# A GNN and FFN kernel on one Trainium2 core: the order of additions, weight loads and a branch around the last projection block and the last stores

## The chip, the cores and the metric

The kernel runs on one core of one Trainium2 chip. The metric is the time of the device in microseconds (us); lower is better. The engines carry these names in the profile: PE is TensorE's matrix multiply and PEld its weight load, DVE is VectorE, ACT is ScalarE, POOL is GpSimd, SP is SyncE, which here issues most of the DMAs. The "span" of a profiled execution goes from its first to its last instruction. L594 means line 594 of the kernel before.

## What is computed

Four residual stages over 1250 nodes with 1024 features each. The reference, cut to its frame:

```python
x = x + _L0_gnn_ref(_layernorm(x), W, a_l, a_r, src, dst)       # graph attention, 4 heads
x = x + _L0_ffn_ref(_layernorm(x)[None], maker, up, w_cproj)[0] # block-diagonal up, gelu, 16384 -> 1024
x = x + _L1_gnn_ref(_layernorm(x), edge_index, W, b)            # graph convolution
x = x + _L1_ffn_ref(_layernorm(x)[None], w1s, w2s, w3s, W1, W2, W3, Wg)[0]  # shared expert + best of 8
```

The second stage ends in `h @ w_cproj.T`, a product of 1250 x 16384 by 16384 x 1024 in float32. It takes most of the time. The third stage begins with `x @ W.T + b`. In the fourth, `shared = gelu(x @ w1s) * (x @ w2s) @ w3s` is added for every node, and to it the output of the one expert that the node chose.

## The kernel before

**The projection.** The long product is cut along its 16384 hidden features into 16 blocks (`NB`), and each block is multiplied by a two-level Strassen-Winograd scheme: 7 outer products, each of 7 inner ones. One step of the loop over `steps` is one product. In blocks 0 to 14 a step has 8 matrix multiplies (L594). Its result lies in one of two PSUM buffers (`po2`), ACT copies it to SBUF (L603, in `accumulate`) into one of five rotating buffers (`parts`, which the profile shows as `low`), and POOL adds it by an accumulating DMA to an array in DRAM, `acc_d` (L607). `acc_d[p, i]` thus gathers inner product i of outer product p over blocks. The operands are sums of weights and of hidden features, which DVE forms (L587, `add_up`).

**The last block.** It has 28 steps, four for each outer product p, which come in the order `OUTER` = 1, 2, 6, 7, 4, 5, 3. Each step takes two pairs of operands, so 16 multiplies. Three things happen beside them:

- `load_sums(p)` brings the seven sums of outer product p back from DRAM with seven DMAs on SP (L622, 313 KB each). `sums_of` names the step at which each p is loaded, counted from the block's first step (`end`): -13, -6, 1, 5, 12, 15, 20. Buffers for them come from those that the operands and the rotating copies leave free.
- `outer_sums(p)` is a generator of seven DVE additions (L629), which turn the seven inner sums into the four quarters of outer product p.
- `combine(p, i, po)` adds the step's PSUM result to that quarter (L643), and combines quarters of several p into the result `xT` (L648). It frees the PSUM buffer. As there are two, the products of step k+2 wait for the combine of step k.

In what order DVE meets additions and combines is decided by the loop: at each step, before the combine of the step before, it pulls two additions from the list `fill` (nine at every fourth step of the last block). A scheduler then fixes the order on each engine, in which each engine runs its instructions one after another.

**Weights of the convolution.** From step 14 of block 15 in the program's order, the sixteen pieces of the third stage's weights (`W3`, 256 KB each) are loaded by POOL (L749) whenever an operand buffer is free, and its bias by L751. The loads are in POOL's queue together with the accumulating DMAs. `W3` is read by `linear` (L775). The transposes of the first tile of nodes, by which the third stage begins (L153, L679), stand among the last products.

**The end.** The experts' outputs are copied from PSUM (L990) and stored by SP to `ys_d` in DRAM. Then a flag is loaded on every engine (L1003), and a branch (L1004) treats the case that an expert was chosen by more nodes than it has room for. With these inputs it is not taken. After the branch POOL gathers each node's expert output (L1040, ten tiles of 125 nodes, `yg` <- `ys_d`). For each tile, `project` multiplies the shared expert's hidden layer by w3s (L998, eight PE records, two PSUM buffers `po7`), DVE adds it to X (L1001), adds X to `yg` (L1046), and SP stores `yg` in two parts (L105, L106).

Of the kernel before, what the change touches and what calls it, by code (L numbers as in the profile page):

```python
# [1 line left out]

# [95 lines left out]
def gnn_ffn_kernel(ctx, tc, x, src, dst, gat_w, a_l, a_r, maker, up, cproj,  # L98
# [439 lines left out]
    with ExitStack() as tail:  # L538
# [61 lines left out]
        def accumulate(b, p, i, po):  # L600
            part = YS[parts[0]]
            parts.append(parts.pop(0))
            nc.scalar.copy(part, po[:, :, :NQ])  # L603
            if b == 0:
                nc.gpsimd.dma_start(acc_d[p - 1, i - 1], part)
            else:
                nc.gpsimd.dma_start(out=acc_d[p - 1, i - 1], in_=part, accum_op=ALU.add)  # L607

        def late_tile(t):
            xn = scratch[:R, (4 + t % 2 * 2) * 512:][:, :D]  # L610
# [7 lines left out]
        def load_sums(p):  # L618

            for i in (2, 3, 4, 5, 1, 6, 7):  # L620
                acc[p, i] = early.pop() if early and p in (1, 2, 4) else place_y(True)
                nc.sync.dma_start(YS[acc[p, i]], acc_d[p - 1, i - 1])  # L622

        def outer_sums(p):

            a = {i: acc.pop((p, i)) for i in INNER}
            for d, x, op, y in ((2, 1, ALU.add, 2), (6, 1, ALU.add, 6), (7, 6, ALU.add, 7), (4, 7, ALU.subtract, 4),
                                (6, 6, ALU.add, 5), (3, 6, ALU.add, 3), (5, 7, ALU.add, 5)):
                tt(YS[a[d]], YS[a[x]], YS[a[y]], op=op)  # L629
                yield  # L630
            for i, j in (("11", 2), ("12", 3), ("21", 4), ("22", 5)):
                acc[p, i] = a[j]
            for j in (1, 6, 7):
                free_acc(a[j])
# [5 lines left out]

        def combine(p, i, po):
            v = YS[acc[p, i]]
            tt(v, po[:, :, :NQ], v, op=ALU.add)  # L643
            a = {q: acc[q, i] for q in OUTER if (q, i) in acc}
            for d, x, op, y in {2: (("11", 1, ALU.add, 2),), 6: ((6, 1, ALU.add, 6),), 7: ((7, 6, ALU.add, 7),),
                                4: (("21", 7, ALU.subtract, 4),), 5: (("22", 7, ALU.add, 5), (5, 6, ALU.add, 5)),
                                3: (("12", 5, ALU.add, 3),)}.get(p, ()):
                tt(output(d, i) if isinstance(d, str) else YS[a[d]], YS[a[x]], YS[a[y]], op=op)  # L648
            for q in {2: (2,), 6: (1,), 4: (4,), 5: (7, 6), 3: (5, 3)}.get(p, ()):
                free_acc(acc.pop((q, i)))  # L650
# [44 lines left out]
        later = dict(zip((33, 36, 38, 40, 42, 44, 46, 48), pieces))  # L695
        late = {1: 5, 2: 6, 3: 7, 4: 8, 5: 9}
        end = (NB - 1) * 49
        last, j, fill, sums_of = None, 0, [], dict(zip((end + v for v in (-13, -6, 1, 5, 12, 15, 20)), OUTER))
        norm = {}
        for n, (b, p, i, pairs) in enumerate(steps):  # L700
            m = n - 49 * b
# [28 lines left out]
                if m in later:  # L730
                    hidden(b + 1, *later[m])
            assert n != end - 13 or all(v < 33 for k, v in buf.items() if k[1] == "X")
            if n in sums_of:
                load_sums(sums_of[n])
                fill.append(outer_sums(sums_of[n]))
            if n == end:
                blocks.close()
                tl = rest.enter_context(tc.tile_pool(name="tl", bufs=2))
# [1 line left out]
                yh += parts  # L740
            if b == NB - 1:
                if m >= 14 and len(W3) < 2 * KD:
                    for g in range(2):
                        for k in range(KD):
                            at = [v for v in xw if not 8 <= v < 16]
                            if at and (k, g) not in W3:
                                xw.remove(at[0])
                                W3[k, g] = XS[at[0]].rearrange("p q o -> p (q o)")
                                nc.gpsimd.dma_start(W3[k, g], gcn_w[k * P:(k + 1) * P, g * 512:(g + 1) * 512])  # L749
                if m == 23:  # L750
                    nc.gpsimd.dma_start(bias, gcn_b.partition_broadcast(R))  # L751
                while m >= 16 and len(fetched) < 4 and fetch(len(fetched)):
                    pass
                if m == 22:
                    add_out(0)
                    level(0)
                if m == 24:
                    turn_tile(0)
                if m == 27:
                    add_out(1)  # L760
                    level(1)
            po = product(pairs)
            for _ in range(9 if n >= end and m % 4 == 3 else 2):
                if n > end - 9 and fill and next(fill[0], 0) == 0:
                    fill.pop(0)
            if last:
                (combine if last[0] == NB - 1 else accumulate)(*last[last[0] == NB - 1:])
            last = b, p, i, po
        combine(*last[1:])

# [99 lines left out]
    with back_end:  # L870
# [120 lines left out]
                        nc.sync.dma_start(ys_d[:NE * ROWS, :].rearrange("(p s) d -> s p d", s=NS)[e * (ROWS // P) + s][:m], y[:m])  # L991

        with tc.tile_pool(name="ops7", bufs=2, space=PSUM) as ops:
            def project(dst, w3t, h, t):
                po = ops.tile([R, 2, 512], F32, name="po7")
                for f in range(2):
                    for g in range(2):
                        nc.tensor.matmul(po[:, g, :], h[:, f, t * R:(t + 1) * R],  # L998
                                         w3t[:, f, g * 512:(g + 1) * 512], start=(f == 0), stop=(f == 1))
                xs = X[:, t, :]  # L1000
                nc.vector.tensor_tensor(xs, po.rearrange("p a b -> p (a b)"), xs, op=ALU.add)  # L1001

            if_late = nc.values_load(flag[0:1, 0:1], min_val=0, max_val=1)  # L1003
            with tc.If(if_late > 0):  # L1004
                with tc.tile_pool(name="lw", bufs=1) as lwp, tc.tile_pool(name="lps", bufs=1, space=PSUM) as lps:
                    for e in range(NE):
                        a, b, c = w1[e], w2[e], w3[e]
                        w12 = lwp.tile([P, 2, KD, F], F32, name="lw12")
                        w3t = lwp.tile([P, 2, D], F32, name="lw3")
                        nc.sync.dma_start(w12[:, 0], a.rearrange("(k p) f -> p k f", p=P))  # L1010
                        nc.sync.dma_start(w12[:, 1], b.rearrange("(k p) f -> p k f", p=P))
                        nc.sync.dma_start(w3t, c.rearrange("(k p) o -> p k o", p=P))
                        mask = lwp.tile([P, N], F32, name="mask")
                        for t in range(T):
                            pb = lps.tile([P, R], F32, name="lpb")
                            nc.tensor.transpose(pb, late[:, t, e:e + 1].to_broadcast([R, P]), ident[:R, :R])
                            nc.scalar.copy(mask[:, t * R:(t + 1) * R], pb)
                        h = lwp.tile([P, 2, N], F32, name="lhid")
                        for f in range(2):
                            for n0, nn in NCH:  # L1020
                                ps = []
                                for i in range(2):
                                    pab = lps.tile([P, 512], F32, name=f"lpab{i}")
                                    for k in range(KD):
                                        nc.tensor.matmul(pab[:, :nn], w12[:, i, k, f * P:(f + 1) * P],
                                                         xT5[:, k, n0:n0 + nn], start=(k == 0), stop=(k == KD - 1))
                                    ps.append(pab)
                                g = lwp.tile([P, 417], F32, name="lg2")
                                nc.scalar.activation(g[:, :nn], ps[0][:, :nn], AF.Gelu)
                                nc.vector.tensor_tensor(g[:, :nn], g[:, :nn], mask[:, n0:n0 + nn], op=ALU.mult)  # L1030
                                nc.vector.tensor_tensor(h[:, f, n0:n0 + nn], ps[1][:, :nn], g[:, :nn], op=ALU.mult)
                        for t in range(T):
                            project(X, w3t, h, t)

            out_t = out.rearrange("(t p) d -> t p d", p=R)
            with tc.tile_pool(name="yg", bufs=T) as ygp:
                ygs = []
                for t in range(T):
                    yg = ygp.tile([R, D], F32, name="yg")
                    nc.gpsimd.indirect_dma_start(  # L1040
                        out=yg, out_offset=None, in_=ys_d,
                        in_offset=bass.IndirectOffsetOnAxis(ap=back[:, t:t + 1], axis=0))
                    ygs.append(yg)
                for t in range(T):
                    project(X, wsh[1], hs, t)
                    nc.vector.tensor_tensor(ygs[t], ygs[t], X[:, t, :], op=ALU.add)  # L1046
                    dma(nc.sync, out_t[t], ygs[t])


# [29 lines left out]
```

## Time and profile before

| what | value |
|---|---|
| time, median of 3 runs | 2980.59 us (2980.43 to 2981.76) |
| profiled execution, its own time | 2978.19 us |
| its span, mean granted PE clock | 2976.5 us, 0.993 |
| busy: PE, DVE, ACT, POOL | 2900.6, 1595.5, 874.9, 764.3 us |
| step of the last block on PE | 4.22 us (16 multiplies of 128x313) |
| one addition on DVE (L629, L643) | 0.81 us |
| accumulating DMAs (L607), issue to landing | 735 of 313 KB, median 5.9 us |
| gathers (L1040), issue to landing | 10, 7.7 / 11.8 / 19.0 us (least, median, most) |

The table by stages lists the busy time of each engine within a stretch, then PE's granted clock, the share of the 16 DMA engines and the bytes moved. In this view of the profile, the stretch from 2200 to 2250 us is the first part of the last block:

```profile
core 0: us, PE busy (x) PEld busy (x) DVE busy (x) ACT busy (x) POOL busy (x), PEclk, DMA share, GB/s
...
2150.00:2200.00 50.00, 49.86 (x225) 32.04 (x224) 29.07 (x43) 23.30 (x35) 19.57 (x26) 1.00 1.02 243
2200.00:2250.00 50.00, 35.55 (x128) 25.07 (x127) 35.02 (x45) 0.00 (x0) 2.28 (x4) 0.86 0.45 137
2250.00:2300.00 50.00, 50.00 (x191) 35.87 (x190) 32.22 (x43) 0.00 (x0) 3.23 (x6) 1.00 0.51 154
```

Around the branch the profile shows these records (PEldq and DVEq are the engines' sequencers; durations in ns, then the time of the start):

```profile
L1004 PEldq COMPARE_BRANCH  x1: 3645/3645/3645, 2927.8 to 2927.8; - x1
L1004 DVEq COMPARE_BRANCH  x1: 68/68/68, 2930.8 to 2930.8; - x1
L1004 PEldq EVENT_SEMAPHORE  x1: 51/51/51, 2931.5 to 2931.5; - x1
L1004 DVEq EVENT_SEMAPHORE  x1: 21/21/21, 2933.6 to 2933.6; - x1
```

### The profile page before, as it was taken

Reading aid. Unit: us, or ns where it says so; the run is one execution under the profiler, and the core shown is the slowest. Engines: PE = TensorE matmul, PEld = TensorE weight load, DVE = VectorE, ACT = ScalarE, POOL = GpSimd, SP = SyncE. Lnnn points to the kernel's source line nnn. Section 1 sums busy time; section 2 is a strip of 40 time slices with the busy share of each in tenths; the row PEclk is TensorE's granted clock in tenths of the full one; section 3 lists DMA queues with packets and bytes.
Section 4 is the critical chain, followed back from the end, with each engine's and each line's share of the span. In section 5 each row is a group of like instructions: output and inputs, shape, how many; then the busy total and the mean of one; then the engine's idle time right before and its main releaser. Section 6 shows DMA issues by size and latency. Waiting matters only on the chain. (4 is left out here: it accounts for less than half of the span.)

```text
span 2976.5 us, 32458 instructions
## 1 busy us (share of the span) xinstructions
PE 2900.6 (97%) x11479; PEld 1914.0 (64%) x11479; DVE 1595.5 (54%) x2611; ACT 874.9 (29%) x1415; POOL 764.3 (26%) x982
## 2 busy tenths in 40 slices
PE   8999899999999999999999999999989999999998
PEld 5574677666766766766766766766757544445774
DVE  7686987846646646646646646645556431221214
ACT  1221234444344344344344344344320110000000
POOL 2010000234434434434433434434320000002001
PEclk9999999999999999999999999999999999999999
DMA  5245523569999999999999999999983202212654
GB/s 141 65 118 140 152 66 125 186 165 172 198 170 172 199 172 170 198 172 171 197 173 171 197 172 171 197 173 148 226 226 115 74 0 74 62 56 85 211 198 164
DMA packets 252548, 449.57 MB, mean 151 GB/s; under 512 B 48160, under 2 KB 132218, under 8 KB 251753
## 3 DMA queue, kind: packets, MB, share of 16 engines
q0 software_dynamic: 115216, 270.53, 53.0%
q1 hardware_dynamic: 137162, 176.86, 19.9%
q8 instruction: 96, 1.57, 0.2%
q14 instruction: 74, 0.61, 0.1%
HBM read 175.38 MB, written 271.89 MB: 150 GB/s over the span
## 5 line engine op out<-in xcount | busy, mean ns | idle before, releaser
L607 POOL DMA_DIRECT2D acc_d<-low x686 | 594.3, 867 | 904.9 <-ACT low L603 875.4
L603 ACT COPY low<-po 128x626 f32<-128x626 f32 x735 | 500.4, 681 | 996.4 <-PE po L594 821.2
L594 PE MATMUL po<-X,arena 128*128 128x313 f32 x2176 | 613.7, 429 | 0.1
L594 PEld LDWEIGHTS po<-X,arena 128*128 128x128 f32 x2176 | 408.3, 190 | 173.4 <-issue 19.9
L594 PE MATMUL po<-low,arena 128*128 128x313 f32 x1552 | 440.2, 429 | 14.4 <-DVE arena L643 14.4
L594 PEld LDWEIGHTS po<-low,arena 128*128 128x128 f32 x1552 | 291.4, 190 | 137.0 <-DVE arena L643 14.9
L594 PE MATMUL po<-X,first_w 128*128 128x313 f32 x840 | 240.0, 428 | 0.0
L594 PE MATMUL po<-X,BZ 128*128 128x313 f32 x720 | 207.3, 431 | 0.0
L594 PEld LDWEIGHTS po<-X,first_w 128*128 128x128 f32 x840 | 157.6, 189 | 66.5 <-issue 6.8
L848 PE MATMUL ph<-low,first_w 125*125 125x512 f32 x400 | 173.6, 593 | 1.4 <-issue 1.4
L594 PEld LDWEIGHTS po<-X,BZ 128*128 128x128 f32 x720 | 135.7, 191 | 57.5 <-issue 7.5
L587 DVE TENSOR_TENSOR X<-X 128x626 f32<-128x626 f32 x141 | 114.2, 812 | 100.2 <-PE po L594 99.8
L594 PE MATMUL po<-low,first_w 128*128 128x313 f32 x560 | 160.6, 429 | 0.0
L209 PE MATMUL pz<-W,xT 128*125 128x512 f32 x320 | 141.2, 595 | 0.2 <-PEq L322 0.2
L594 PE MATMUL po<-low,BZ 128*128 128x313 f32 x480 | 138.4, 428 | 0.0
L848 PEld LDWEIGHTS ph<-low,first_w 125*125 125x125 f32 x400 | 74.2, 188 | 94.8 <-issue 94.8
L594 PEld LDWEIGHTS po<-low,first_w 128*128 128x128 f32 x560 | 104.6, 190 | 44.2 <-issue 5.5
L587 DVE TENSOR_TENSOR X<-low,X 128x626 f32<-128x626 f32 x101 | 82.0, 816 | 83.8 <-PE po L594 81.6
L587 DVE TENSOR_TENSOR low<-X 128x626 f32<-128x626 f32 x102 | 82.8, 815 | 69.4 <-PE po L594 69.1
L587 DVE TENSOR_TENSOR X<-X,low 128x626 f32<-128x626 f32 x92 | 75.1, 818 | 80.4 <-PE po L594 80.1
L277 PE MATMUL pc<-os,od 125*125 125x417 f16 (+1 forms) x588 | 110.9, 345 | 5.0 <-issue 5.0
L448 PE MATMUL po<-BZ,w 125*125 125x257 f32 x400 | 96.6, 401 | 18.7 <-DVE w L446 17.4
(263 smaller groups left out, 3407.2 us busy)
## 6 DMA issues: line engine op xcount, KB each, us to landing
acc_d<-low POOLq DMA_DIRECT2D x735, 313.0 KB, 5.9
arena<-in_cproj SPq DMA_DIRECT2D x148, 256.0 KB
w<-in_w SPq DMA_DIRECT2D x16, 1024.0 KB
BZ<-in_cproj SPq DMA_DIRECT2D x56, 256.0 KB
first_w<-in_cproj SPq DMA_DIRECT2D x52, 256.0 KB
nm<-nm_d SPq DMA_DIRECT2D x20, 546.9 KB
w3t<-in_w SPq DMA_DIRECT2D x8, 1024.0 KB
X<-acc_d SPq DMA_DIRECT2D x21, 313.0 KB
```

Source lines behind the costliest of these rows:

```text
L209: nc.tensor.matmul(pz, xT[:, k, t * R:(t + 1) * R], W[g][:, k], start=(k == 0), stop=(k == KD - 1))
L277: nc.tensor.matmul(pc[:, b, :nn], od[:, d - near[c][0], :], os[:, n0:n0 + nn], start=(c == win[d][0]), stop=(c == win[d][-1]))
L448: nc.tensor.matmul(po[i], w[:, i * R:(i + 1) * R], Z[h // 2][:, s, h % 2, :], start=(s == 0), stop=(s == T - 1))
L587: tt(view(k), *a, op=ALU.add if sign == "+" else ALU.subtract)
L594: nc.tensor.matmul(po[:, o, :NQ], view(x)[:, q, o * P:(o + 1) * P], view(y)[:, q, :], start=(i == q == 0), stop=(i + 1 == len(pairs) and q ...
L603: nc.scalar.copy(part, po[:, :, :NQ])
L607: nc.gpsimd.dma_start(out=acc_d[p - 1, i - 1], in_=part, accum_op=ALU.add)
L848: nc.tensor.matmul(pa[:, g, :], cs[:, c, :], Hs[:, c, g * 512:(g + 1) * 512], start=(c == 0), stop=(c == T - 1))
```

## The change

Three parts.

1. *Additions of the last block's sums.* The list `fill` and its loop are gone. A list `bring` says for each outer product from which step on its additions run, and how many per step: from -9 two, 0 two, 3 two, 10 four, 14 four, 18 three, 22 three, for p in the order `OUTER`. They come after the step's combine in the program, and for steps after `end` they are tied behind it: `tc.issue_after(added[-1])` places what is within it after the last combine's L643 in the order of the engine. The fourth sum (p=7) is loaded at step 7 instead of 5.
2. *Weights of the convolution.* The loads of `W3` are placed after the last accumulating DMA (`sent[0]`).
3. *The overflow branch.* The load of the flag and the branch stand after the gathers, the projections and the stores. `project` gets the place that it adds to as an argument. Within the branch, the late nodes' output is added to `ygs` instead of X, and all tiles are stored once more.

```diff
-                nc.gpsimd.dma_start(out=acc_d[p - 1, i - 1], in_=part, accum_op=ALU.add)
+                sent[:] = [nc.gpsimd.dma_start(out=acc_d[p - 1, i - 1], in_=part, accum_op=ALU.add).ins]
...
-            tt(v, po[:, :, :NQ], v, op=ALU.add)
+            added.append(tt(v, po[:, :, :NQ], v, op=ALU.add).ins)
...
-        last, j, fill, sums_of = None, 0, [], dict(zip((end + v for v in (-13, -6, 1, 5, 12, 15, 20)), OUTER))
+        last, j = None, 0
+        loads_at = dict(zip((end + v for v in (-13, -6, 1, 7, 12, 15, 20)), OUTER))
+        bring = [(end + v, k, outer_sums(w)) for v, k, w in zip((-9, 0, 3, 10, 14, 18, 22), (2, 2, 2, 4, 4, 3, 3), OUTER)]
+        added, sent = [], []
...
-            if n in sums_of:
-                load_sums(sums_of[n])
-                fill.append(outer_sums(sums_of[n]))
+            if n in loads_at:
+                load_sums(loads_at[n])
...
-                    for g in range(2):
-                        for k in range(KD):
+                    for g, k in [(g, k) for g in range(2) for k in range(KD)]:
+                        with tc.issue_after(sent[0]):
...
             po = product(pairs)
-            for _ in range(9 if n >= end and m % 4 == 3 else 2):
-                if n > end - 9 and fill and next(fill[0], 0) == 0:
-                    fill.pop(0)
             if last:
                 (combine if last[0] == NB - 1 else accumulate)(*last[last[0] == NB - 1:])
+            for n0, k, sums_of in bring:
+                if n0 <= n:
+                    with tc.issue_after(added[-1]) if n > end else nullcontext():
+                        for _ in range(k):
+                            next(sums_of, None)
...
-            def project(dst, w3t, h, t):
+            def project(w3t, h, t, dst):
...
-                xs = X[:, t, :]
-                nc.vector.tensor_tensor(xs, po.rearrange("p a b -> p (a b)"), xs, op=ALU.add)
-
-            if_late = nc.values_load(flag[0:1, 0:1], min_val=0, max_val=1)
-            with tc.If(if_late > 0):
...
-                            project(X, w3t, h, t)
+                nc.vector.tensor_tensor(dst, po.rearrange("p a b -> p (a b)"), dst, op=ALU.add)
...
-                    project(X, wsh[1], hs, t)
+                    project(wsh[1], hs, t, X[:, t, :])
                     nc.vector.tensor_tensor(ygs[t], ygs[t], X[:, t, :], op=ALU.add)
                     dma(nc.sync, out_t[t], ygs[t])
+
+                if_late = nc.values_load(flag[0:1, 0:1], min_val=0, max_val=1)
+                with tc.If(if_late > 0):
...
+                            for t in range(T):
+                                project(w3t, h, t, ygs[t])
+                    for t in range(T):
+                        dma(nc.sync, out_t[t], ygs[t])
```

The order of each engine's instructions after the change can be known without running it, and the prediction uses it.

More of the change, by code (lines that the diff above doesn't have):

```diff
@@ L1 @@
-from contextlib import ExitStack
+from contextlib import ExitStack, nullcontext
 import concourse.bass as bass
@@ L999, in project @@
                                          w3t[:, f, g * 512:(g + 1) * 512], start=(f == 0), stop=(f == 1))
-                xs = X[:, t, :]
-                nc.vector.tensor_tensor(xs, po.rearrange("p a b -> p (a b)"), xs, op=ALU.add)
-            if_late = nc.values_load(flag[0:1, 0:1], min_val=0, max_val=1)
[L1004 to L1032, printed above, removed]
-                            project(X, w3t, h, t)
@@ L1044, in gnn_ffn_kernel @@
                 for t in range(T):
-                    project(X, wsh[1], hs, t)
+                    project(wsh[1], hs, t, X[:, t, :])
                     nc.vector.tensor_tensor(ygs[t], ygs[t], X[:, t, :], op=ALU.add)
                     dma(nc.sync, out_t[t], ygs[t])
+                if_late = nc.values_load(flag[0:1, 0:1], min_val=0, max_val=1)
+                with tc.If(if_late > 0):
+                    with tc.tile_pool(name="lw", bufs=1) as lwp, tc.tile_pool(name="lps", bufs=1, space=PSUM) as lps:
+                        for e in range(NE):
+                            a, b, c = w1[e], w2[e], w3[e]
+                            w12 = lwp.tile([P, 2, KD, F], F32, name="lw12")
+                            w3t = lwp.tile([P, 2, D], F32, name="lw3")
+                            nc.sync.dma_start(w12[:, 0], a.rearrange("(k p) f -> p k f", p=P))
+                            nc.sync.dma_start(w12[:, 1], b.rearrange("(k p) f -> p k f", p=P))
+                            nc.sync.dma_start(w3t, c.rearrange("(k p) o -> p k o", p=P))
+                            mask = lwp.tile([P, N], F32, name="mask")
+                            for t in range(T):
+                                pb = lps.tile([P, R], F32, name="lpb")
+                                nc.tensor.transpose(pb, late[:, t, e:e + 1].to_broadcast([R, P]), ident[:R, :R])
+                                nc.scalar.copy(mask[:, t * R:(t + 1) * R], pb)
+                            h = lwp.tile([P, 2, N], F32, name="lhid")
+                            for f in range(2):
+                                for n0, nn in NCH:
+                                    ps = []
+                                    for i in range(2):
+                                        pab = lps.tile([P, 512], F32, name=f"lpab{i}")
+                                        for k in range(KD):
+                                            nc.tensor.matmul(pab[:, :nn], w12[:, i, k, f * P:(f + 1) * P],
+                                                             xT5[:, k, n0:n0 + nn], start=(k == 0), stop=(k == KD - 1))
+                                        ps.append(pab)
+                                    g = lwp.tile([P, 417], F32, name="lg2")
+                                    nc.scalar.activation(g[:, :nn], ps[0][:, :nn], AF.Gelu)
+                                    nc.vector.tensor_tensor(g[:, :nn], g[:, :nn], mask[:, n0:n0 + nn], op=ALU.mult)
+                                    nc.vector.tensor_tensor(h[:, f, n0:n0 + nn], ps[1][:, :nn], g[:, :nn], op=ALU.mult)
+                            for t in range(T):
+                                project(w3t, h, t, ygs[t])
+                    for t in range(T):
+                        dma(nc.sync, out_t[t], ygs[t])
```

## The prediction

> **What bounds the kernel now.** The page gives TensorE 97% of the 2976.5 us span, so I did not ask which engine is busy but where TensorE is not. First the groups of instructions: almost every product group has an idle time of 0.0 or 0.1 us, one has 14.4.
>
> ```profile
> L594 PE MATMUL po<-low,arena 128*128 128x313 f32 x1552 | 440.2, 429 | 14.4 <-DVE arena L643 14.4
> ```
>
> Then the timeline of PE around it. Columns: start, duration, instruction, and in brackets the idle time before it with its releaser.
>
> ```profile
> 2200.58 1.22 PE L594 MATMUL po<-X,BZ 128*128 128x313 f32 x4
> 2216.24 2.46 PE L594 MATMUL po<-low,arena 128*128 128x313 f32 x4 [14.45 <-DVE arena L643]
> 2218.49 1.91 PE L594 MATMUL po<-X,arena 128*128 128x313 f32 x4
> 2220.24 1.22 PE L594 MATMUL po<-low,arena 128*128 128x313 f32 x4
> 2221.29 1.22 PE L594 MATMUL po<-X,arena 128*128 128x313 f32 x4
> 2222.35 1.22 PE L594 MATMUL po<-low,first_w 128*128 128x313 f32 x4
> ```
>
> The reader is to see two losses: the gap, and after it groups of 2.46 and 1.91 us where 1.22 is normal. This step took 2222.35 - 2216.24 = 6.11 us; the others take 4 x 1.055 = 4.22. Next, why L643 was late: VectorE's timeline.
>
> ```profile
> 2200.59 1.66 DVE L629 TENSOR_TENSOR X<-X 128x626 f32<-128x626 f32 x2 [8.58 <-DMA X<-acc_d]
> 2202.79 1.73 DVE L629 TENSOR_TENSOR X<-X 128x626 f32<-128x626 f32 x2 [0.55 <-DMA X<-acc_d]
> ...
> 2214.66 0.81 DVE L629 TENSOR_TENSOR X<-X 128x626 f32<-128x626 f32 x1
> 2215.38 0.80 DVE L643 TENSOR_TENSOR arena<-po,arena 128x626 f32<-128x626 f32 x1
> ```
>
> The first combine had its product at about 2197.5, but runs at 2215.38, behind L629 additions that wait for loads. On the engine's order 16 of them stand between the last L587 addition for the first step and this combine: five of p=2, six of p=6, five of p=7. Those loads are late for a reason on POOL, whose timeline is next.
>
> ```profile
> 2175.48 0.86 POOL L607 DMA_DIRECT2D acc_d<-low  x1 [1.25 <-ACT low L603]
> 2186.40 0.58 POOL L749 DMA_DIRECT2D arena<-in_gcn_w  x1 [10.06 <-DVE arena L587]
> ...
> 2199.78 0.87 POOL L607 DMA_DIRECT2D acc_d<-low  x1 [2.57 <-DMA arena<-in_gcn_w]
> ```
>
> A W3 load waits 10.06 us for VectorE with the last seven accumulations behind it; the last goes out at 2199.78. Five loads of p=6 need those accumulations landed, as they reuse their buffers.
>
> The windows table shows no other such place: from 2250 to 2920 us PE is busy nearly throughout. So time won here is not given back on the way, and the next place that counts is the tail:
>
> ```profile
> 2933.76 36.02 PE L998 MATMUL po<-w3s,hs 128*125 128x512 f32 x80 [4.23 <-DVEq L1004]
> ```
>
> [...] 2.46 us against 1.22 after the 14.45 us gap. [...] accumulations and loads crowd one another, windows 2150 to 2200 have a DMA share of 1.02, and accumulations land after 7.3 us there, 5.9 over the kernel. [...] The trace has DVE's compare at 2930.8 and its next event at 2933.6, 2.8 us; PE's compare lasts 3.645 us.
>
> **The change, part by part.** Sums are made against the profiled execution's 2978.19 us (span 2976.5). The median of the runs is 2.40 us higher, and I subtract the same gain from it.
>
> *Additions behind combines.* Nothing is removed: 49 additions of 0.81 us stay. In the changed order on DVE the first combine goes ahead of the last five L629 of p=2, and no addition of p=6 precedes combine 2. PE's steps end at 2197.4, 2201.8, 2206.0, 2210.2, 2214.4; step k+2 needs combine k. Combine 0 is done by about 2198.3, needed at 2201.8. Then the third sum of p=2 waits for a load (2200.6 as before, if not earlier), four additions of 0.81 end at 2203.9, combine 1 at 2204.7, needed at 2206.0. Three additions and combine 2 end at 2207.9, needed at 2210.2.
> Now the critical one: the first addition of p=6 stands before combine 3 and waits for the load into the buffer that the very last accumulation used. That accumulation goes out at about 2194.1 (product ends 2193.0, ACT copy 0.68, hand-over 0.4), lands 6 to 7.3 us later at 2200 to 2201.4; the load then needs 4 to 8 us on crowded engines: 2205 to 2209. VectorE gets there at 2208.7, does four operations (3.3 us), and combine 3 ends at 2212.8, needed at 2214.4. So the load may land at about 2210 without a pause. Later steps carry two to four additions (at most 3.2 us), a combine (0.8) and up to two L648; I find slack of 1.7 to 3 us at the tightest (steps 10 and 15).
> Gain: the gap of 14.45 plus the slow clock, 6.11 - 4.22 = 1.89: **16.3 us**. If the load is late, the pause is its lateness, 0 to 4 us, plus 1.9 if the clock falls. Below nothing: the load order moves as well (the fourth sum's seven loads two steps, 8.4 us, later), but its first use is step 10, some 13 us after.
>
> *W3 behind the last accumulation.* It is this that brings the last accumulation from 2199.78 to about 2194.1; taken into the sum above. On POOL all seven accumulations now precede the sixteen L749 issues (0.54 to 0.6 us each) and the bias. W3 is first used by L775 at about 2331, more than 130 us after the first eight loads went out in the trace of before (2186 to 2197), so their delay of up to 8 us is hidden; the later ones wait for buffers as before. About seven W3 loads then meet the p=6 loads on the 16 engines (256 KB; by the page's queue table 176.86 MB took 19.9% of the span, so 0.9 us each): at most 6.3 us, which is the upper end of the lateness above.
>
> *Overflow branch behind the stores.* It was not taken: it costs the flag's load, the compare and the jump. PE no longer waits 4.23 us, nor restarts slowly (the first four weight loads are 0.86 us apart, not 0.43: 1.7 us). By the changed order half of tile 0 fills the 1.32 us hole ahead of the last expert's second half (L987 at 2925.86), so that ends 0.3 us later. But the next limit is near. The gathers (L1040) wait for the last ys_d store, not for the branch: gather 0 went out at 2935.06, landed at 2942.98; now 2943.4. DVE's order is X0, X1, yg0, X2, yg1, yg2, X3, and po7 has two buffers: tile 4's products wait for X2, which stands behind yg0. X2 ends at 2943.4 + 2 x 1.2 = 2945.8; yg2 waits for gather 2 (2948.9), so X3 ends at 2951.3, tile 5 starts there, and five tiles of 3.43 end at 2968.5 where before they ended at 2969.79. Gain **1.3 us** of some 6. Bounds: -2 if the new pauses cost a slow clock once more and the branch shows, +3 if gathers land sooner. At the end the branch (2.8 us from yg9's end on DVE) lies beside the last store's landing (3.3 us after it: issue at 0.02 and 0.38 us, landing until 2975.6), so it costs nothing; without this cover it would be up to 2 us.
>
> Sum: 16.3 + 1.3 = 17.6 us. Span 2976.5 to 2958.9; median 2980.59 to **2963.0**.
>
> **Rivals.**
> (a) *The gap only moves.* Loads of p=6 or p=7 are DMA-bound, and combine 3 and its followers pause 5 to 10 us in all, slow clock included. For: DMA share 1.02 before the place, and in the trace of before a load issued at 2191.31 landed at 2200.59. Against: the W3 loads leave the crowded stretch, and the share falls to 0.45 after 2200. It gives 2968 to 2973.
> (b) *The tail gains all.* The gathers land early enough not to count: 4.2 + 1.7 us instead of 1.3: 2958.5. Against: gather 0 was the releaser of 2.84 us of DVE's idle time already.
> (c) *Slower.* Tying makes each sum's last load wait for an addition that itself stands behind a combine, so that SP's in-order queue serves every sum one step too late. Price: a load's 9.3 us (2191.31 to 2200.59) less the one step of 4.2 that two po buffers cover, 5.1 us, plus 1.9 of slow clock, at five sums (6, 7, 4, 5, 3) = 35 us, against 17.6: 2998. It decides from (17.6 + 6)/5 = 4.7 us a sum. Against: before, the later combines wait for PE (L643 <- PE 2.42 us), not for loads.
> (d) *The tie does not hold*: additions still stand ahead of a combine, and a gap of the same length opens elsewhere: no change, 2975 to 2981. Against: the order on DVE.
>
> **How the numbers follow.** Forecast 0.66, (a) 0.16, (b) 0.06, (c) 0.06, (d) 0.06. Own range of the forecast: 2959.5 to 2967 (lateness 0 to 4, tail -2 to +3). Including (b) and most of (a): **2959 to 2971.5**. A measurement of this kernel can tell 0.2%, 6 us, from no change. Faster: 0.66 + 0.16 + 0.06 = 0.88; same: 0.06; slower: 0.06.
>
> **What would show it.** PE without a gap over 2 us between 2190 and 2300, no 2.46 us group, first transposes of tile 0 about 16 us earlier; the first L643 near 2197.5 ahead of any p=6 addition; seven L607 in a row before L749, the last near 2194; the wait of the first p=6 addition ending before 2210. In the tail: no idle time put down to the branch, but idle time of L998 with DVE X L1001 as releaser behind gather 0. The prediction is wrong if PE's idle time returns at combines 3 to 15, or if SP's or PE's queue waits at the branch after the last store.

## The result and the profile after

The changed kernel takes 2961.02 us (median of 4 runs, 2960.31 to 2961.79), the kernel before beside it 2980.51 us. The ratio is 0.9935, with a 95% interval of 0.9918 to 0.9952. That is 19.5 us, or 0.65%, faster. The forecast was 2963.0 us and a range of 2959 to 2971.5. The profiled execution took 2961.70 us with a span of 2959.9; the sum of the prediction had put its span at 2958.9.

First PE's timeline of the changed kernel at the place of the old gap (start, duration, instruction, idle time before):

```profile
2200.57 1.22 PE L594 MATMUL po<-X,BZ 128*128 128x313 f32 x4
2201.63 1.22 PE L594 MATMUL po<-low,arena 128*128 128x313 f32 x4
2202.68 1.22 PE L594 MATMUL po<-X,arena 128*128 128x313 f32 x4
2203.74 1.22 PE L594 MATMUL po<-low,arena 128*128 128x313 f32 x4
```

The step that had started at 2216.24 starts at 2201.63, with no idle time and at 1.22 us a group: gap and slow clock are both gone. In the table by stages the stretch has full PE and full clock:

```profile
2200.00:2250.00 50.00, 50.00 (x191) 35.88 (x190) 38.59 (x51) 0.00 (x0) 2.15 (x4) 1.00 0.50 167
```

VectorE's timeline of the changed kernel shows why:

```profile
2197.61 0.81 DVE L643 TENSOR_TENSOR arena<-po,arena 128x626 f32<-128x626 f32 x1 [9.53 <-PE po L594]
...
2206.78 0.80 DVE L629 TENSOR_TENSOR X<-X 128x626 f32<-128x626 f32 x1
2208.67 0.81 DVE L629 TENSOR_TENSOR low<-low 128x626 f32<-128x626 f32 x1 [1.09 <-DMA low<-acc_d]
...
2211.56 0.80 DVE L643 TENSOR_TENSOR arena<-po,arena 128x626 f32<-128x626 f32 x1
```

The first combine now waits for PE alone. The first addition of p=6 (2208.67) waits for its load, but only 1.09 us, and combine 3 behind it (2211.56) ends at 2212.4, some 2 us before PE asks for its buffer (2214.29). POOL's timeline, and a row of SP's queue after it, show the way of this load: seven accumulations without a W3 load between them, the last at 2194.40 instead of 2199.78; SP waits for it to land (2.2 us put down to `acc_d<-low`) and issues the load at 2201.68; VectorE uses it 7.0 us later.

```profile
2191.36 0.86 POOL L607 DMA_DIRECT2D acc_d<-low  x1 [1.25 <-ACT low L603]
2194.40 0.86 POOL L607 DMA_DIRECT2D acc_d<-low  x1 [2.18 <-ACT low L603]
2194.99 0.85 POOL L751 DMA_DIRECT2D BZ<-in_gcn_w  x1
```

```profile
2201.68 0.32 SPq L622 DMA_DIRECT2D low<-acc_d  x1
```

In the tail the branch is no longer a releaser, but PE is not free of waits. PE's timeline, then VectorE's (L1002 is the product in `project`, before L998; L1004 the addition to X, before L1001; L1017 the addition to yg, before L1046):

```profile
2912.03 12.18 PE L1002 MATMUL po<-w3s,hs 128*125 128x512 f32 x28
2927.97 3.70 PE L1002 MATMUL po<-w3s,hs 128*125 128x512 f32 x8 [3.76 <-DVE X L1004]
2934.31 17.43 PE L1002 MATMUL po<-w3s,hs 128*125 128x512 f32 x40 [2.64 <-DVE X L1004]
```

```profile
2925.55 1.23 DVE L1017 TENSOR_TENSOR yg<-yg,X 125x1024 f32<-125x1024 f32 x1 [6.95 <-DMA yg<-ys_d,back]
2926.70 1.22 DVE L1004 TENSOR_TENSOR X<-po,X 125x1024 f32<-125x1024 f32 x1
...
2931.89 1.22 DVE L1017 TENSOR_TENSOR yg<-yg,X 125x1024 f32<-125x1024 f32 x1 [2.73 <-DMA yg<-ys_d,back]
2933.04 1.22 DVE L1004 TENSOR_TENSOR X<-po,X 125x1024 f32<-125x1024 f32 x1
```

Two pauses, 6.4 us, stand where one of 4.23 was. Their releaser is the addition to X, which on DVE stands behind a yg addition that waits for a gather.

The last yg addition ends at 2954.27, and the span 5.63 us later; before the change it was 4.20 us. The records of the branch (L1021) and, after them from another view, those of SP's closing waits at the end of the program (L1080):

```profile
L1021 SPq EVENT_SEMAPHORE  x8: 17/17/17, 2955.3 to 2958.2; - x8
...
L1021 PEldq COMPARE_BRANCH  x1: 3874/3874/3874, 2947.5 to 2947.5; - x1
...
L1021 DVEq COMPARE_BRANCH  x1: 68/68/68, 2954.2 to 2954.2; - x1
L1021 SPq COMPARE_BRANCH  x1: 53/53/53, 2955.1 to 2955.1; - x1
L1021 DVEq EVENT_SEMAPHORE  x1: 21/21/21, 2957.6 to 2957.6; - x1
```

```profile
L1080 SPq EVENT_SEMAPHORE  x14: 17/28/28, 2958.3 to 2959.8; - x14
```

The same closing records in the kernel before (there at L1075):

```profile
L1075 SPq EVENT_SEMAPHORE  x14: 17/28/28, 2973.1 to 2976.4; - x14
```

Before, SP's closing waits begin at 2973.1, right after the issue of the last store (2972.69), and nine of the 14 are through by 2973.6, while the store is still under way (it lands at 2975.4). Now SP comes to the branch first. Behind it the last store's landing is waited for (until 2958.2), and only then do the closing waits begin. DVE's jump, from 2954.2 to 2957.6, ends before that.

**One yardstick for all kernels.** Runs of one kernel differ by some us in the long part ahead of the last block (with additions and W3 loads changed, the first row below starts at 2190.72 us in one execution and at 2195.43 in the other). So each profiled execution is cut at two rows of PE's timeline: the start of the last small product L428 (2189.82 before) and the start of the last expert's first product with w3 (2920.95 before). "Middle" lies between, "tail" is from there to the end of the span, and "last" is the part of the tail after the end of the last yg addition. All are in us; the end of the span is known to 0.05 us. Where a kernel was profiled twice, both are given.

| kernel | middle | tail | last |
|---|---|---|---|
| before | 731.13 | 55.55 | 4.20 |
| changed (2 executions) | 713.21, 713.22 | 56.46, 56.29 | 5.63, 5.72 |
| additions alone | 719.36 | 55.92 | 4.20 |
| W3 loads alone | 729.92 | 55.78 | 4.14 |
| branch alone | 731.12 | 56.20 | 5.42 |
| additions and W3 loads (2) | 713.22, 713.22 | 56.06, 57.55 | 4.20, 4.15 |
| changed, no tie | 727.89 | 54.96 | 5.39 |
| changed, p=6 one step sooner | 715.05 | 55.92 | 5.65 |
| changed, no branch (2) | 713.22, 713.23 | 54.84, 54.21 | 4.21, 4.16 |
| changed, other order in the tail (2) | 713.22, 713.23 | 53.77, 53.58 | 6.39, 6.31 |

The middle repeats within 0.02 us, the tail within about 1.5 us. All of the gain that these traces show, 17.9 us, is in the middle. The tail shows none. Of the 1.5 us between the two tails of additions and W3 loads, 1.1 lies in the slow products behind the wait at the branch (4.48 and 4.23 us): in the second trace the eighth product with w3s starts 5.86 us after the first and not 4.77. In the kernel before, behind its wait of 4.23 us, the granted clock is 0.66 from 2934 to 2938 us.

### The profile page after: what moved, and what is told of

It reads as the page before. It is cut to its first block, busy times and chain, and to the rows that moved or that the text cites. A ratio compares the mean times of both kernels' runs of the same rounds, so it can differ in the third digit from the quotient of the medians.

```text
span 2959.9 us, 32455 instructions
## 1 busy us (share of the span) xinstructions
PE 2896.8 (98%) x11479; PEld 1911.6 (65%) x11479; DVE 1593.2 (54%) x2611; ACT 875.9 (30%) x1415; POOL 764.1 (26%) x982
## 4 chain that ended last, share of the span: by engine, by line
PE 83%; DVE 1%; DMA 1%; ACT 0%; issue 0%; POOL 0%; DVEq 0%; ACTq 0%
PE po L594 56%; PE ph L852 6%; PE pab L885 6%; PE po L779 5%; PE pz L428 3%; PE po L448 3%; PE po L991 2%; PE po L1002 1%; PE pt L153 1%; DMA low<-acc_d 1%; PE pg L840 1%; DMA yg<-ys_d,back 0%; DMA rowbd<-st 0%; PE px L679 0%; PE pt L981 0%
## 5 line engine op out<-in xcount | busy, mean ns | idle before, releaser
L448 PE MATMUL po<-BZ,w 125*125 125x257 f32 x400 | 96.6, 401 | 19.5 <-DVE w L446 18.2
```

The source lines that it names most:

```text
L448: nc.tensor.matmul(po[i], w[:, i * R:(i + 1) * R], Z[h // 2][:, s, h % 2, :], start=(s == 0), stop=(s == T - 1))
```

## The experiments

**Each part by itself.** The first three runs take one part of the change each and leave the rest of the kernel before; the fourth leaves out the third part.

The additions alone:

```diff
-            tt(v, po[:, :, :NQ], v, op=ALU.add)
+            added.append(tt(v, po[:, :, :NQ], v, op=ALU.add).ins)
...
-            for _ in range(9 if n >= end and m % 4 == 3 else 2):
...
+            for n0, k, sums_of in bring:
+                if n0 <= n:
+                    with tc.issue_after(added[-1]) if n > end else nullcontext():
...
```

> Only the additions are changed; the W3 loads and the branch stay as before. Theory (additions and W3 loads work as a pair): the last accumulation still goes out at about 2199.8 behind a W3 load that waits for DVE, its landing holds the load that the first addition of p=6 needs until about 2214, so combine 3 is late by some 4 us: PE shows a pause of 3 to 6 us between 2210 and 2225 and a slow clock after it; 2967 to 2972 us. Rival (the order on DVE is the whole cause): no pause over 1 us in the last block; 2962 to 2965 us.

Measured 2967.92 us, ratio 0.9959 (0.9946 to 0.9973). PE's and DVE's timelines of this kernel:

```profile
2216.93 1.71 PE L594 MATMUL po<-low,arena 128*128 128x313 f32 x4 [3.36 <-DVE arena L643]
2218.43 2.29 PE L594 MATMUL po<-X,BZ 128*128 128x313 f32 x4
```

```profile
2213.17 0.81 DVE L629 TENSOR_TENSOR low<-low 128x626 f32<-128x626 f32 x1 [6.48 <-DMA low<-acc_d]
```

The theory holds. With the W3 loads still between the accumulations, the last of them goes out at 2198.13, the load that p=6 needs is issued at 2208.28 and used at 2213.17 (counted from the start of the middle, 24.7 us instead of 18.4), and combine 3 makes PE pause 3.36 us; the clock falls (the next groups take 1.71 and 2.29 us, not 1.22). The middle is 6.1 us longer than with both parts.

The W3 loads alone:

```diff
-                    for g in range(2):
-                        for k in range(KD):
+                    for g, k in [(g, k) for g in range(2) for k in range(KD)]:
+                        with tc.issue_after(sent[0]):
```

> Only the W3 loads are changed. Theory: 16 additions still stand ahead of the first combine; their loads come some 5 us sooner, so the gap ahead of step 2 shrinks from 14.45 to 8 to 11 us, the slow clock after it stays; 2974 to 2978 us. Rival (POOL's blocked queue is the whole cause): gap under 3 us; 2963 to 2966 us.

Measured 2979.31 us, ratio 0.9998 (0.9990 to 1.0006): nothing. This is a miss of the theory's size too: the gap shrank to 12.55 us, not to 8 to 11, and the middle by 1.2 us.

```profile
2201.12 3.50 DVE L629 TENSOR_TENSOR X<-X 128x626 f32<-128x626 f32 x4 [6.41 <-DMA X<-acc_d]
...
2213.16 0.81 DVE L643 TENSOR_TENSOR arena<-po,arena 128x626 f32<-128x626 f32 x1
```

The last accumulation went out at 2194.08, as early as in the changed kernel, but the additions ahead of the first combine now waited for loads into X. What held those, the waits of SP's queue between 2165 and 2215 us show:

```profile
SPq L622 <- DVE X L629: 21.4, 3, 12.2
```

SP waited up to 12.2 us at a time for earlier additions to free an X buffer. So POOL's blocked queue was the cause that came last in the trace of before, with another just behind it.

The branch alone, put behind the loop that stores:

```diff
-            if_late = nc.values_load(flag[0:1, 0:1], min_val=0, max_val=1)
-            with tc.If(if_late > 0):
...
                     dma(nc.sync, out_t[t], ygs[t])
+
+                if_late = nc.values_load(flag[0:1, 0:1], min_val=0, max_val=1)
+                with tc.If(if_late > 0):
```

> Only the branch is moved. Theory (the gathers take the branch's place and the branch shows at the end): PE idles about 6 us in the projections of the tail with additions to X as releaser, the last PE product ends 0.5 to 1 us sooner than before, the end after the last addition is 1 to 1.5 us longer; 2979.5 to 2982 us, no change that can be told. Rival (the branch was on the path with all its 4.2 us of gap and 1.7 of slow clock): 2974 to 2976 us.

Measured 2978.60 us, ratio 0.9991 (0.9983 to 0.9999). The time is 0.9 us below the theory's range and does not reach the rival's. The interval ends just under 1, so the time hints at a gain of 2 us; the profiled execution, the slowest of the 13, has a tail of 56.20 us against 55.55 and doesn't show where it would be.

Additions and W3 loads together, with the branch where it was: the first two diffs in one kernel.

> Additions and W3 loads changed, the branch left where it was. Theory: the last block's gain is all of the gain, 17 us; 2962 to 2964 us, no PE pause over 1 us from 2190 to 2320, PE's wait of 4.2 us at the branch as before. Rival (the tail brought part of the 19.5 us between the medians): 2965 to 2968 us.

Measured 2962.39 us, ratio 0.9941 (0.9928 to 0.9955). The theory holds: without the branch's move nearly all of the gain is there. Parts one and two gain 11.8 and 1.2 us of middle by themselves and 17.9 together.

**The tie and the steps.** Two runs change only where additions stand on DVE.

```diff
 e5: -  with tc.issue_after(added[-1]) if n > end else nullcontext():
     +  with nullcontext():
 e8: -  (-9, 0, 3, 10, 14, 18, 22)
     +  (-9, 0, 2, 10, 14, 18, 22)
```

> The changed kernel with the additions in the same steps of the program but not tied behind the last combine; on DVE the first combine then stands behind six more additions, two of them of p=6. Theory (the order on DVE against the landing of the p=6 loads decides): combine 0 waits for a p=6 load, about 2204, where PE needs it at 2201.6, and combine 1 stands behind the last p=6 load (2208.7 in the changed kernel): pauses of 4 to 8 us in all ahead of steps 2 and 3 and a slow clock; 2966 to 2972 us. Rival (the steps in the list and the W3 order suffice, the tie is idle): 2960 to 2962 us, no pause.

Measured 2972.53 us, ratio 0.9974 (0.9965 to 0.9983), just above the theory's range; the rival is out. The scheduler puts additions of p=6 ahead of combine 0:

```profile
2211.05 0.81 DVE L629 TENSOR_TENSOR X<-low,X 128x626 f32<-128x626 f32 x1 [13.51 <-DMA X<-acc_d]
2211.90 0.81 DVE L629 TENSOR_TENSOR X<-X 128x626 f32<-128x626 f32 x1
2212.62 0.80 DVE L643 TENSOR_TENSOR arena<-po,arena 128x626 f32<-128x626 f32 x1
```

One addition that waits 13.51 us for its load makes a gap of 11.27 us on PE, for which I had 4 to 8: I had this load land at 2204, and it was used at 2211.05. The list of steps, the W3 order and the later load of p=7 are thus worth 3.2 us of middle together, the tie the other 14.7. What the later load of p=7 does by itself was not tried.

> The changed kernel with the additions of p=6 from step 2 on instead of 3, so that the wait for their last load stands ahead of combine 2, still tied. Theory: the load lands at about 2208.7 as before, combine 2 ends near 2212.5, PE needs it at 2210.1: one pause of 2 to 3.5 us ahead of step 4, with or without a slow clock; 2963 to 2966 us. Rival (later steps have slack that takes it up, or the loads come sooner when asked for sooner): 2960.5 to 2961.5 us.

Measured 2963.59 us, ratio 0.9943 (0.9929 to 0.9956). PE's timeline of it:

```profile
2213.70 1.32 PE L594 MATMUL po<-low,arena 128*128 128x313 f32 x4 [1.47 <-DVE arena L643]
```

There is one pause, ahead of step 4 as expected, but of 1.47 us and not 2 to 3.5, with a middle 1.8 us longer; the clock stays (the group takes 1.32 us, the next 1.22). The time's interval covers both answers, the trace decides for the theory. One step (4.2 us) of delay is what keeps the wait off PE, with about 2 us to spare.

**The tail.** One run leaves the branch with all that is in it out, one (e7) changes the order of additions:

```diff
 e7: for t in range(T):
         project(wsh[1], hs, t, X[:, t, :])
+    for t, s in enumerate((3, 4, 5, 6, 7, 7, 8, 9, 9, 9)):
+        with tc.issue_after(shared[s]):      # the addition to X of tile s
             nc.vector.tensor_tensor(ygs[t], ygs[t], X[:, t, :], op=ALU.add)
         dma(nc.sync, out_t[t], ygs[t])
```

```diff
 e6: -  if_late = nc.values_load(flag[0:1, 0:1], min_val=0, max_val=1)
     -  with tc.If(if_late > 0):
...
```

> The changed kernel without the load of the flag and the overflow branch: the case that an expert has more nodes than room is left out. Theory (the branch at the end shows by 1 to 1.5 us after the last addition): 2959.3 to 2960.2 us, and from the end of the last yg addition to the end of the span 4.2 us instead of 5.6. Rival (the last store's landing hides the branch, as the prediction had it): 2960.7 to 2961.3 us, the same as the changed kernel.

Measured 2959.43 us, ratio 0.9930 (0.9917 to 0.9944). The last part is 4.21 us instead of 5.63: the branch at the end costs 1.4 us. The time alone can't tell this. Without the branch, in both traces, the last store lands 3.1 us after the first of its two issues and the span ends 1.0 us after the landing, as in the kernel before. In all traces with the branch at the end it is 1.8 us after the landing, because SP's closing waits come only then: that is some 0.75 us of the 1.4. The rest is that the store itself lands later, 3.6 to 3.9 us after its issue in the five traces with this order of additions. Why it does is not shown; while the store is under way (2954.29 to 2958.1) the changed kernel's trace has two DMA packets of an instruction queue, where the trace before has none.

> The changed kernel with the tail's additions to yg tied behind later additions to X (yg0 after X3, yg1 after X4, and so on), so that X2 and X3 no longer stand behind gathers. Theory (the gathers stall PE only through the order on DVE; behind it the 16 DMA engines, full from 2922 to 2947, are the next bound): no pause of PE in the tail, its last product ends 6 us sooner, but the last addition only 3 to 4.5 us sooner as it waits for gathers; 2956.5 to 2958.5 us. Rival 1 (the DMA engines are already the bound of the tail): under 1 us gained, 2960 to 2961 us. Rival 2 (all of PE's 6.4 us is gained): 2954.5 us.

Measured 2959.74 us, ratio 0.9931 (0.9917 to 0.9944), which is between the theory and its first rival. The traces speak more plainly. PE's timeline, and DVE's last row:

```profile
2914.72 32.78 PE L1004 MATMUL po<-w3s,hs 128*125 128x512 f32 x76
```

```profile
2952.28 1.23 DVE L1021 TENSOR_TENSOR yg<-yg,X 125x1024 f32<-125x1024 f32 x1 [1.26 <-DMA yg<-ys_d,back]
```

PE runs through without a pause and ends 41.4 us after the start of the tail instead of 48.3, so 6.9 sooner. But the last addition waits 1.26 us for its gather and ends only 3.45 us sooner, and the last store lands 4.6 us after its issue, so that the tail is 2.7 us shorter: 53.77 against 56.46. The gathers are then the bound.

**The four of the tail again, on one chip.** Here the changed kernel stands beside three of the others.

> The changed kernel once more, so that it stands beside the next three on one chip. Theory (the moved branch gains next to nothing: PE's idle time behind the gathers and the branch at the end eat what the old place had cost): from the start of the last expert's first product with w3 to the end of the span about 56.5 us, as in the first trace (56.46), and 0 to 1.5 us from the kernel with the branch left in place. Rival (the move is worth the 1.3 us of the prediction or more): 2 us or more below it.

> Additions and W3 loads changed, the branch left in place, once more. Theory: 2961.5 to 2963.5 us, the same stretch at the end about 56 us (56.06 in the first trace). Rival as for the run beside it.

> The changed kernel without the flag and the branch (the overflow case is left out), once more. Theory: the branch at the end costs 1.4 us: 1 to 2 us below the changed kernel, from the last yg addition to the end 4.2 us again. Rival: no difference.

> The changed kernel with the tail's yg additions behind later X additions, once more. Theory: 2 to 3 us below the changed kernel, the stretch at the end about 53.8 us as in the first trace, no PE pause in it, last yg addition waiting for a gather. Rival (the difference was the run's, not the kernel's): within 1 us of the changed kernel.

Medians of 5: changed 2962.57, branch left in place 2962.20, no branch 2960.08, other order 2961.14 us; the ratios to before are 0.9942, 0.9938, 0.9935 and 0.9935, each with an interval of about 0.0013 to either side. No branch lies 2.5 us below the changed kernel and the other order 1.4, where 1 to 2 and 2 to 3 were expected, but the runs of one kernel spread by 3 to 9 us: the times can't tell these four apart. The tails repeat, but for the second: 56.29, 57.55, 54.21 and 53.58 us. Together with the tails of all kernels with the branch in its old place (55.55 to 57.55) and of the complete ones with it at the end (54.96 to 56.46, the other order apart), a gain from moving the branch is not shown; the hint of 2 us from the run with the branch alone stays open. By the traces the order of yg behind X is worth 2.7 us on top of the change, so that kernel is the best complete one by its trace; by its time it is not shown to be.

## Why the prediction was right

- *Additions behind combines, with W3 behind the last accumulation, 16.3 us.* Measured 17.9 in the middle. The two terms of the sum were there (gap 14.45, slow clock 1.89) and nothing came back: after step 2 PE has no idle time until 2330, and the first tile's transposes start at 2295.38 instead of 2312.84. Of the 1.6 us too few, 0.82 is PE's wait at these transposes (L153), of which the prediction said nothing; it went, and why stays open. The rest, 0.8 us, lies in small differences around the gap.
- *The critical load.* Said to land at 2205 to 2209 (its 4 to 8 us under way were an estimate) and to be harmless until 2210; it was used at 2208.67. The last accumulation, said 2194.1, went out at 2194.40, and the load, issued 7.3 us after it, took 7.0 us at most. Rival (a) had this margin right as the risk: one step sooner, or with the W3 loads in the way, the pause comes (1.47 and 3.36 us).
- *W3 behind the last accumulation, "taken into the sum".* As a part of a pair it is worth 6.1 us, alone 1.2.
- *Overflow branch behind the stores, 1.3 us.* This is the term that was mis-sized. The chain on PE was as told: tiles 4 and 5 stop behind yg0 and yg2. The last product ends 0.5 us sooner (48.30 us after the start of the tail, before 48.83), where I had 1.3: X3 ended 0.5 us later in the tail than I had it, and the last five tiles took 17.43 us instead of 17.15. What failed is the step that the branch "lies beside the last store's landing", "so it costs nothing": it costs 1.4 us (5.63 against 4.20, and 4.21 with the branch left out). I had priced DVE's jump alone, 2.8 us; it took 3.4 and did lie beside the landing. I had left out SP, whose closing waits used to pass during the landing and now follow it, and the store's own landing, 3.8 us after its issue instead of 3.1. The prediction had named SP's queue waiting at the branch after the last store as a sign of being wrong; for this term the sign is there.
- *The sum.* The tail by the trace is 0.9 us longer, within the bounds of -2 to +3 given, and no more than two traces of one kernel differ. Middle 17.9, tail -0.9 and 0.4 us that the part before the middle was longer make the 16.6 us between the two spans, where the sum had 17.6. That it came so close is in part luck: the middle was 1.6 us better and the tail 2.2 us worse than said. Between the medians it is 19.5 us, as the two profiled executions lay 2.3 us below and 0.7 us above their medians. The forecast's own range, 2959.5 to 2967, doesn't follow from the bounds written beside it either: +3 instead of +1.3 in the tail gives 2961.3 at the least, and a load 4 us late with -2 in the tail gives 2970.3. The measured 2961.02 lies just under the first of these.
- *Rival (b), the tail gains all.* Not seen: it needs another order on DVE, and even then the gathers leave only 2.7 us of it. *Rival (c), each sum one step too late.* Not seen: no combine after step 2 makes PE wait. *Rival (d), the tie does not hold.* The tie holds, and without it 14.7 us of the middle return.
- Left open: why the runs of one kernel differ by up to 9 us (2958.99 to 2967.99 for additions and W3 loads, 2976.44 to 2985.48 for the kernel before). In seven of the eleven traces with part one an addition of p=1 waits longer for its load and PE pauses 0.2 to 4 us near 2155 us. VectorE's order there is the same before and after the change. In the traces without part one this pause did not appear, but there are only three of those; so it isn't excluded that part one costs something here, outside the middle.

## What to carry to other kernels

Where the fixed order of one engine holds both a consumer that waits for slow loads and a step that frees another engine's buffer (in the kernel before, DVE's additions waited up to 8.58 us for loads, and the combine behind them came at 2215.38), put the second first and tie it there, because here the list of steps without the tie didn't hold the scheduler to it (14.7 us); then check for how many steps the load may be late (here one of 4.2 us, with about 2 us to spare). The wait in a queue of stores (here a weight load in POOL's) was worth removing only with the order behind it, 6.1 us of middle against 1.2: alone it uncovered the next wait. And before moving a wait at the end of a program, price what stands second: here, by the traces, the gathers (6.4 us of pauses on PE where one of 4.23 had been) and the new place's own cost (1.4 us) took back all that the branch had.

## What the runs showed of the hardware that was not expected

In these traces nearly the same pause cost a slow clock or did not. In the tail, 3.76 us of idle time was followed by eight products in 3.70 us in one execution of the changed kernel (shown above; granted clock 1.00 from 2917 to 2947 us), and in the other 3.80 us of idle time by the same eight in 5.39 us (0.94 in the same stretch):

```profile
2929.18 5.39 PE L1002 MATMUL po<-w3s,hs 128*125 128x512 f32 x8 [3.80 <-DVE X L1004]
2935.23 17.43 PE L1002 MATMUL po<-w3s,hs 128*125 128x512 f32 x40 [0.66 <-DVE X L1004]
```

It made no difference there, since the next tile waits for its gather anyway (0.66 instead of 2.64 us). In the seven traces that have this pause, of 3.49 to 3.80 us, the clock fell in four and stayed in three, and not by length: after 3.49 the granted clock from 2917 to 2947 us is 0.89, after 3.79 it is 1.00. In the last block pauses of 3.36, 11.27, 12.55 and 14.45 us slowed the clock (the slowest group of four products behind them took 2.29, 2.45, 2.46 and 2.46 us), one of 1.47 us did not (1.32 us). In the kernel before the granted clock is 0.50 from 2216 to 2219 us, behind the pause of 14.45. What decides it for the pauses of about 3.5 us is not shown.

A branch whose body is skipped takes time in these traces, though its compare lasts only 0.07 us on DVE: from there to DVE's next record it is 2.8 to 4.6 us, and PE's compare itself lasts 3.4 to 5.9 us, in part beside PE's last products. At the end of the changed kernel it was neither of these that set the end (PE's next record is at 2951.8, DVE's at 2957.6), but what SP had to do behind the branch (from 2958.3 to 2959.8).
